# Splitting an expert's 176 hidden units as 128 and 48, and running the down matmuls of tiles in pairs

## The chip, the cores and the metric

The kernel runs on one NeuronCore of one Trainium2 chip. The metric is the device time of one execution in microseconds. Three runs of the kernel before gave 1685.27, 1688.10 and 1691.52 us; the median is 1688.1. A profile is of one further execution.

## The reference, cut to what matters

The model is a two-layer decoder on an input of 16 sequences of 128 tokens, width 256, all in float32. Layer 0 is self-attention with 16 heads, a recurrent mixing over time, and a mixture of experts; layer 1 is self-attention, cross-attention and a quantised feed-forward. The change touches the mixture of experts of layer 0 alone. For each token `h` it computes

```
top4   = the 4 best of 16 experts by router weight
out    = sum over e in top4 of  wt[e] * ( silu(h @ w_gate[e]) * (h @ w_up[e]) ) @ w_down[e]
         + sigmoid(h . sh_gate_w) * ( silu(h @ sh_gate) * (h @ sh_up) ) @ sh_down
w_gate[e], w_up[e]: 256 x 176      w_down[e]: 176 x 256
sh_gate, sh_up:     256 x 704      sh_down:   704 x 256
```

The second line is a "shared expert" that every token goes through. The 176 hidden units of an expert are what the change splits in another way: they are the contracted dimension of the last product, and TensorE contracts over partitions[...].

## The kernel before

The kernel walks through the layers in stages. In the expert stage the tokens have been scattered to a DRAM buffer `hs`, sorted by expert and padded, and a map `tmapT` holds for each of 79 tiles of 128 rows the expert (row 0 of the map) and the first row in `hs` (row 1). 79 is 16 * 4 + 16 - 1 (`NTILES`), the most that the padding can need. Each tile takes five functions:

- `fetch(j)` (L741 to L750) reads the tile's row number from the map into a register of SyncE and lets SyncE's queue load 128 rows from `hs` into `hx`, which has four buffers.
- `turn_in(j)` (L936) transposes `hx` on TensorE into PSUM (`pht`, L940), and ScalarE copies it to `hxT` (L942).
- `inner(j)` (L946) multiplies `hxT` by the expert's gate and up weights, which lie together in `wbig` and are addressed with the expert number in a register of TensorE (`pgu`, L956). ScalarE takes the silu of one half (L961), VectorE multiplies by the other (`eact`, 128 x 176, L963).
- `turn_act(j)` (L966) transposes `eact` in two halves of 88 columns (`pat`, L970), and VectorE copies both with one instruction to `eactT` (L972).
- `outer(j)` (L975) multiplies `eactT` by the expert's down weights (`pey`, L979), two matmuls with 88 rows each that add up in PSUM. ScalarE or VectorE copies the result to `ey` (L985), and SyncE's queue stores it to `hs` in place of the input rows (L987).

All weights of all experts are loaded once, ahead of the stage: gate and up to `wbig` (L689), down to `wd` (L695) as 88 partitions x 16 experts x 2 halves x 256.

The order on TensorE is written out by hand (`manual_schedule`): the loop over steps `s` calls, in this order, `fetch(s)`, `turn_in(s-2)`, `inner(s-3)`, `turn_act(s-5)`, `outer(s-6)` and then `beside(s)`.

```python
for s in range(NTILES + LAG):
    for f, lag in ((fetch, 0), (turn_in, 2), (inner, 3), (turn_act, 5), (outer, LAG)):
        if 0 <= s - lag < NTILES and not (f is fetch and s in where):
            f(s - lag)
    beside(s)
```

`beside(s)` puts other work between the tiles: up to three "chores" a step at first (loads and quantising of layer 1's weights, on VectorE, ScalarE, GpSimd and SyncE's queue), from step 27 on the gathers of finished rows by GpSimd (`back_rows`) and their sums (`back_sums`), and from step 36 on, every second step, a piece of layer 1's self-attention. The other engines' orders are a scheduler's.

The four tiles in PSUM that these functions write (`pht`, `pgu`, `pat`, `pey`) share one pool, `tps`, of four buffers of a bank each, given out in turn; whoever takes a buffer waits until its last content has been read.

One other place matters. The shared expert (`sh_hidden`, `sh_down`, L701 to L735) runs just before, and its 704 units are five chunks of 128 and one of 64. For that one the kernel already puts 64-row matmuls on two row groups of TensorE in turn: partitions 0 to 63 and 64 to 127 (the last chunk of `acc_sh`, L728).

Of the kernel before, what the change touches and what calls it, by code (L numbers as in the profile page):

```python
# [9 lines left out]
F32 = mybir.dt.float32  # L10
# [7 lines left out]
P = 128  # L18
B = 16
S = 128  # L20
D = 256
NK = D // P
# [7 lines left out]
E = 16  # L30
TOPK = 4
IMOE = 176
# [4 lines left out]
NTILES = B * TOPK + E - 1  # L37
# [15 lines left out]
def decoder(ctx, tc, a, out):  # L53
    nc = tc.nc
    V, A, PE, GP = nc.vector, nc.scalar, nc.tensor, nc.gpsimd
# [42 lines left out]
    for r in range(H // 4):  # L98
        hs = slice(4 * r, 4 * r + 4)
# [7 lines left out]
    ident = const.tile([P, P], F32, name="ident")  # L107
# [9 lines left out]
    ET, SPE = mybir.EngineType.PE, mybir.EngineType.SP  # L117
# [219 lines left out]
    hs = dram.tile([ROWS, D], F32, name="hs")  # L337
# [202 lines left out]
    with tc.tile_pool(name="l0", bufs=2, reuse_waits="tile") as wk0:  # L540
        hTs, qTs, kTs, live, accs, norms = {}, {}, {}, {}, {}, {}
# [117 lines left out]
    tps = psum1.enter_context(tc.tile_pool(name="tps", bufs=4, space=PSUM, reuse_waits="tile"))  # L659
# [14 lines left out]
    mp = moestack.enter_context(tc.tile_pool(name="moe", bufs=3, reuse_waits="tile"))  # L674
# [12 lines left out]
    for k in range(NK):  # L687
        for j, name in ((0, "L0_ffn_w_gate"), (1, "L0_ffn_w_up")):
            nc.sync.dma_start(  # L689
                wgu[:, k, :, j * IMOE : (j + 1) * IMOE], a[name][:, k * P : (k + 1) * P, :].rearrange("e p i -> p e i"),  # L690
            )
    HM = IMOE // 2
    wd = mp.tile([HM, E, 2, D], F32, name="wd", bufs=1)
    for j in range(2):
        nc.sync.dma_start(wd[:, :, j, :], a["L0_ffn_w_down"][:, j * HM : (j + 1) * HM, :].rearrange("e p d -> p e d"))  # L695

# [37 lines left out]

    why = "the map holds each of its candidates once"
    NB = 8
    held, where, live = {}, {}, {}

    def fetch(j):  # L741
        row = nc.values_load(
            tmapT[0:1, 1, j : j + 1], engines=[SPE], min_val=0, max_val=ROWS - P, skip_runtime_bounds_check_because=why,
        )
        where[j] = row
        hx = mp.tile([P, D], F32, tag="hx", name="hx", bufs=4)
        ins = nc.sync.dma_start(hx, hs[bass.ds(row, P), :]).ins
        tc.declare_no_dep(ins, group="stores", reason="each tile has rows of its own")
        tc.add_to_no_dep_group("fetches", ins)
        live[j] = hx  # L750

    tmapT = rt.tile([1, 2, P], I32, name="tmapT")
# [43 lines left out]
    def map_and_first():  # L796
        yield from tile_map()
        while scatters:
            yield UNIT
        for j in range(2):  # L800
            fetch(j)
# [162 lines left out]
        live[j] = act  # L964

    def turn_act(j):  # L966
        act = live[j]
        pt = tps.tile([P, NK, P], F32, tag="t", name="pat")
        for k in range(2):
            PE.transpose(pt[:HM, k, :], act[:, k * HM : (k + 1) * HM], ident)  # L970
        aT = mp.tile([HM, 2, P], F32, tag="eactT", name="eactT")
        V.tensor_copy(aT, pt[:HM])  # L972
        live[j] = aT

    def outer(j):  # L975
        aT = live.pop(j)
        py = tps.tile([P, D], F32, tag="t", name="pey")
        for k in range(2):
            ins = PE.matmul(  # L979
                py, aT[:, k, :], wd[:, bass.ds(held[j], 1), k, :].rearrange("p e d -> p (e d)"),  # L980
                start=k == 0, stop=k == 1,
            )
        last_pe[:] = [ins.ins]
        y = mp.tile([P, D], F32, tag="ey", name="ey")
        nc.any.tensor_copy(y, py)  # L985

        ins = nc.sync.dma_start(hs[bass.ds(where[j], P), :], y).ins  # L987
        for group in ("stores", "fetches", "gathers"):
            tc.declare_no_dep(ins, group=group, reason="each tile has rows of its own")
        tc.add_to_no_dep_group("stores", ins)  # L990

# [6 lines left out]
    moments, rows = {}, {}  # L1000
# [54 lines left out]
    for tag in ("hT3", "hg"):  # L1055
        r = rt.tile([P, 2 * H, 32], F32, tag=tag, name="spread")
# [3 lines left out]
    for i in range(2):  # L1060
        r = xa.tile([P, H, 32], F32, tag=f"vaug{i}", name=f"vaug{i}")
# [232 lines left out]
    with tc.issue_after(sh_down.last):  # L1294
        with tc.manual_schedule(engines={ET}):
# [5 lines that stand above are left out]
            load_last_weights()  # L1301
# [12 lines left out]
    kraw, kTs, vs, qTs, sqs, sums, rqs, live, accs = ({} for _ in range(9))  # L1314
# [314 lines left out]
```

## Time and profile before

| what | value |
|---|---|
| median of three runs | 1688.1 us |
| time of the profiled execution | 1678.52 us |
| its span, first to last instruction | 1676.8 us |
| mean granted TensorE clock | 0.987 |
| TensorE matmuls, busy share of the span | 97% |
| VectorE / ScalarE / GpSimd, busy share | 57% / 49% / 34% |
| expert stage, first to last down matmul | 773.4 to 1028.4 us |
| down matmuls `pey` (L979) | 316 records, 82.6 us busy |
| transposes `pat` (L970) | 158 records, 273 ns median |
| copies `eactT` (L972) | 79, 420 ns median |
| copies `ey` (L985) | 75 on ScalarE, 372 ns median; 4 on VectorE, 425 ns |

How to read the lines of a profile. "PE" is TensorE's matmuls and "PEld" its weight loads, which overlap with them; DVE is VectorE, ACT ScalarE, POOL GpSimd, SP SyncE; an engine's name with a q is its queue of issues. A line of the timeline has the start in us from the beginning of the span, the length in us, the engine, the line of the kernel, the operation, output<-inputs, the shape, and how many instructions are merged in it; in brackets stands how long the engine was idle before, and what it waited for. Matmuls are pipelined and the ends of their records are modelled, so a row's own duration is longer than the place that it takes in the stream; the distance from start to start is what counts. A float32 matmul leaves two weight loads and two matmul records (two passes), a transpose one of each. In a shape such as 88*128 the first number is the rows (contracted), the second the columns of the array that are in use.

### The profile page before, as it was taken

Reading aid. Unit: us, or ns where it says so; the run is one execution under the profiler, and the core shown is the slowest. Engines: PE = TensorE matmul, PEld = TensorE weight load, DVE = VectorE, ACT = ScalarE, POOL = GpSimd, SP = SyncE. Lnnn points to the kernel's source line nnn. Section 1 sums busy time; section 2 is a strip of 40 time slices with the busy share of each in tenths; the row PEclk is TensorE's granted clock in tenths of the full one; section 3 lists DMA queues with packets and bytes.
Section 4 is the critical chain, followed back from the end, with each engine's and each line's share of the span. In section 5 each row is a group of like instructions: output and inputs, shape, how many; then the busy total and the mean of one; then the engine's idle time right before and its main releaser. Section 6 shows DMA issues by size and latency. Waiting matters only on the chain.

```text
span 1676.8 us, 27285 instructions
## 1 busy us (share of the span) xinstructions
PE 1620.3 (97%) x9808; PEld 1149.9 (69%) x9808; DVE 950.3 (57%) x2492; ACT 814.3 (49%) x2208; POOL 569.1 (34%) x586
## 2 busy tenths in 40 slices
PE   8999999999999999989999999999999999999996
PEld 4666666666666675546776667777777777777774
DVE  2333476457547665633355546467666666666756
ACT  3444454444444533403444445656666666665553
POOL 2010132135124233131265345654444444432420
PEclk9999999999999999999999999999999999999998
DMA  9990000000000019132543225000000000000000
GB/s 299 403 358 1 0 7 7 14 25 26 0 20 32 13 46 268 23 96 87 154 149 111 88 89 177 17 14 11 8 8 8 7 8 8 8 8 10 4 4 13
DMA packets 91660, 110.22 MB, mean 66 GB/s; under 512 B 8646, under 2 KB 66950, under 8 KB 91526
## 3 DMA queue, kind: packets, MB, share of 16 engines
q1 hardware_dynamic: 83094, 89.55, 16.5%
q0 software_dynamic: 6144, 16.79, 3.2%
q10 hardware_dynamic: 2288, 2.14, 0.4%
q8 instruction: 78, 1.28, 0.3%
q14 instruction: 56, 0.46, 0.1%
HBM read 54.06 MB, written 54.39 MB: 65 GB/s over the span
## 4 chain that ended last, share of the span: by engine, by line
PE 90%; DVE 3%; issue 3%; ACT 2%; POOL 1%; DMA 0%; POOLq 0%; DVEq 0%; ACTq 0%; SPq 0%
PE proj L571 13%; PE acc_x L1419 6%; PE proj L1353 6%; PE projv L590 6%; PE acc_l L169 6%; PE pgu L956 5%; PE pey L979 4%; PE sc L581 3%; PE sc L1384 3%; PE z L619 3%; PE z L1404 3%; PE acc_sh L728 2%; PE pg L709 2%; PE pu L709 2%; PE pk L1319 2%
## 5 line engine op out<-in xcount | busy, mean ns | idle before, releaser
L184 ACT ACTIVATE sc<-sc,nmax 128x128 f32<-128x128 f32 x512 | 199.0, 390 | 160.3 <-DVE nmax L181 130.3
L181 DVE TENSOR_REDUCE nmax<-sc 128x4 f32<-128x512 f32 x128 | 87.4, 683 | 184.9 <-POOL sc L584 183.3
L584 POOL TENSOR_SCALAR_AFFINE_SELECT sc<-sc 128x512 f32<-128x512 f32 x64 | 40.9, 639 | 330.9 <-ACT sc L583 313.7
L1353 PEld LDWEIGHTS proj<-hc,wbig 128*128 128x128 f32 x1024 | 124.0, 192 | 29.2 <-issue 23.4
L125 POOL TENSOR_TENSOR rq<-rq,mhalf 128x4 f32<-128x4 f32 x64 | 67.8, 1059 | 209.3 <-DVE rq L1376 193.2
L1419 PE MATMUL acc_x<-wbig,zT 128*128 128x256 f32 x512 | 124.8, 386 | 0.7 <-ACT zT L1410 0.7
L1353 PE MATMUL proj<-hc,wbig 128*128 128x128 f32 x1024 | 124.6, 275 | 0.1
L571 PE MATMUL proj<-hT,wq 128*128 128x512 f32 x256 | 122.2, 600 | 0.5 <-ACT hT L156 0.5
L590 PE MATMUL projv<-wv,hT 128*128 128x512 f32 x256 | 122.3, 601 | 0.0
L169 PEld LDWEIGHTS acc_l<-wo,zT 128*128 128x128 f32 x512 | 96.7, 190 | 36.8 <-issue 26.8
L169 PE MATMUL acc_l<-wo,zT 128*128 128x256 f32 x512 | 120.9, 379 | 0.0
L571 PE MATMUL proj<-hT,wk 128*128 128x512 f32 x256 | 120.3, 592 | 0.0
L956 PE MATMUL pgu<-wbig,hxT 128*128 x316 | 108.8, 467 | 2.7 <-DVE eactT L972 1.3
L1419 PEld LDWEIGHTS acc_x<-wbig,zT 128*128 128x128 f32 x512 | 93.3, 190 | 23.6 <-issue 11.3
L125 POOL TENSOR_TENSOR ss<-ss,mhalf 128x32 f32<-128x32 f32 x16 | 87.5, 5471 | 45.3 <-DVE ss L1102 45.2
L1213 POOL DMA_INDIRECT back<-hs,idx x64 | 64.1, 1002 | 93.4 <-DMA hs<-ey 46.2
L184 ACT ACTIVATION_READ_ACCUMULATOR sc<-sc,nmax 128x1 f32 x512 | 95.6, 187 | 0.0
L1387 DVE SCALAR_TENSOR_TENSOR sc<-sc,rq,mask 128x128 f32<-128x128 f32 x256 | 77.4, 343 | 28.6 <-PE sc L1384 24.1
L571 PEld LDWEIGHTS proj<-hT,wk 128*128 128x128 f32 x256 | 48.8, 191 | 61.7 <-issue 53.3
L972 DVE COPY eactT<-pat 88x256 f32<-88x256 f32 x79 | 33.0, 418 | 99.4 <-PE pat L970 79.5
L619 PEld LDWEIGHTS z<-probT,v 128*128 128x128 f32 x512 | 67.1, 192 | 29.5 <-issue 28.7
L979 PE MATMUL pey<-wd,eactT 88*128 x316 | 82.6, 384 | 1.6 <-ACT hxT L942 0.9
(342 smaller groups left out, 3508.8 us busy)
## 6 DMA issues: line engine op xcount, KB each, us to landing
hs<-zero SPq DMA_DIRECT2D x16, 2048.0 KB
hx<-hs SPq DMA_DIRECT2D x79, 128.0 KB
hs<-ey SPq DMA_DIRECT2D x79, 128.0 KB
wbig<-in_L_ffn_w_gate_dram SPq DMA_DIRECT2D x2, 1408.0 KB
wbig<-in_L_ffn_w_up_dram SPq DMA_DIRECT2D x2, 1408.0 KB
wd<-in_L_ffn_w_down_dram SPq DMA_DIRECT2D x2, 1408.0 KB
wq<-in_L_attn_W_Q_dram SPq DMA_DIRECT2D x8, 256.0 KB
vT<-in_ctxT_dram ACTq DMA_DIRECT2D x8, 256.0 KB
```

Of the source, the lines that this page charges most:

```text
L125: power.last = GP.tensor_tensor(v, v, mhalf[:, :n], ALU.pow).ins
L169: ins = PE.matmul(acc[:, t, :], zT[:, i, :], w[:, h0 + i, :], start=h0 == 0 and i == 0 and t % 2 == 0, stop=last and i == 3, skip_group_ch ...
L181: softmax.last = V.tensor_reduce(nmax, sc, AX.X, ALU.max, negate=True).ins
L184: A.activation(p[:, i, :], sc[:, i, :], AF.Exp, bias=nmax[:, i : i + 1], accum_out=rs[:, i : i + 1])
L571: PE.matmul(pj, w[:, k, h, :], hTs[g][:, k, :], start=k == 0, stop=k == NK - 1)
L590: PE.matmul(pv, hTs[g][:, k, at], wv[:, k, 4 * hq : 4 * hq + 4, :].rearrange("p h e -> p (h e)"), start=k == 0, stop=k == NK - 1,)
L619: PE.matmul(pz[:, i, :], v[:, i, :], pT[:, i, :], start=True, stop=True)
L956: PE.matmul(pg, hT[:, k, :], wgu[:, k, bass.ds(held[j], 1), :].rearrange("p e i -> p (e i)"), start=k == 0, stop=k == NK - 1,)
L979: ins = PE.matmul(py, aT[:, k, :], wd[:, bass.ds(held[j], 1), k, :].rearrange("p e d -> p (e d)"), start=k == 0, stop=k == 1,)
L1353: PE.matmul(pj[:, i, :], wqx[:, n, k, i * DH : (i + 1) * DH], hTs[b][:, k, :], start=k == 0, stop=k == NK - 1,)
L1387: V.scalar_tensor_tensor(sc[:, i, :], psc[:, i, :], rq[:, i : i + 1], mask, ALU.mult, ALU.add)
L1419: PE.matmul(accs[b][:, :D], zT[:, i, :], wox[:, 4 * n + i, :], start=n == 0 and i == 0, stop=n == NKV - 1 and i == 3,)
```

## The change

The 176 units of an expert are split as 128 and 48 in place of 88 and 88.

- `wd` now holds only the first 128 units' weights of all experts (128 partitions x 16 x 256), loaded with one DMA.
- The weights of the last 48 units are loaded for each tile by `fetch(j)`: it reads the expert number from the map into a second register and issues one more DMA of 48 rows of 1 KB, ahead of the load of `hx`, into `wd2` with eight buffers. For even tiles they go to partitions 0 to 47, for odd tiles to partitions 64 to 111.
- `turn_act` transposes the first 128 columns of `eact`, and then, for an even tile, the last 48 (which land on partitions 0 to 47), and for an odd tile the last 112, so that the last 48 units land on partitions 64 to 111. VectorE copies in two instructions; `eactT` has four buffers in place of three.
- `outer(j)` does nothing for an even tile, except for the last tile (78). For an odd tile it does the pair: the two 128-row matmuls, then the two 48-row matmuls, which lie on different row groups of TensorE; then two copies and two stores. In the loop the pair's matmuls come in the steps with odd `s`, in which `turn_act` treats an even tile; the steps with even `s` have no down matmuls.

```diff
-    HM = IMOE // 2
-    wd = mp.tile([HM, E, 2, D], F32, name="wd", bufs=1)
-    for j in range(2):
-        nc.sync.dma_start(wd[:, :, j, :], a["L0_ffn_w_down"][:, j * HM : (j + 1) * HM, :].rearrange("e p d -> p e d"))
+
+    HR, HO = IMOE - P, P // 2
+    wd = mp.tile([P, E, D], F32, name="wd", bufs=1)
+    nc.sync.dma_start(wd, a["L0_ffn_w_down"][:, :P].rearrange("e p d -> p e d"))
...
     def fetch(j):
...
         where[j] = row
+        e = nc.values_load(
+            tmapT[0:1, 0, j : j + 1], engines=[SPE], min_val=0, max_val=E - 1, skip_runtime_bounds_check_because=why,
+        )
+        r = j % 2 * HO
+        wds[j] = mp.tile([P, D], F32, tag="wd2", name="wd2", bufs=8)
+        nc.sync.dma_start(wds[j][r : r + HR], a["L0_ffn_w_down"][bass.ds(e, 1), P:].rearrange("e p d -> (e p) d"))
         hx = mp.tile([P, D], F32, tag="hx", name="hx", bufs=4)
...
     def turn_act(j):
-        act = live[j]
-        pt = tps.tile([P, NK, P], F32, tag="t", name="pat")
-        for k in range(2):
-            PE.transpose(pt[:HM, k, :], act[:, k * HM : (k + 1) * HM], ident)
-        aT = mp.tile([HM, 2, P], F32, tag="eactT", name="eactT")
-        V.tensor_copy(aT, pt[:HM])
+        act, r = live[j], j % 2 * HO
+        pt = tps.tile([P, 2, P], F32, tag="t", name="pat")
+        PE.transpose(pt[:, 0, :], act[:, :P], ident)
+
+        PE.transpose(pt[: r + HR, 1, :], act[:, P - r :], ident)
+        aT = mp.tile([P, 2, P], F32, tag="eactT", name="eactT", bufs=4)
+        V.tensor_copy(aT[:, 0, :], pt[:, 0, :])
+        V.tensor_copy(aT[r : r + HR, 1, :], pt[r : r + HR, 1, :])
         live[j] = aT
 
     def outer(j):
-        aT = live.pop(j)
-        py = tps.tile([P, D], F32, tag="t", name="pey")
-        for k in range(2):
-            ins = PE.matmul(
-                py, aT[:, k, :], wd[:, bass.ds(held[j], 1), k, :].rearrange("p e d -> p (e d)"),
-                start=k == 0, stop=k == 1,
-            )
+
+        if j % 2 == 0 and j < NTILES - 1:
+            return
+        js = range(j - j % 2, j + 1)
+        pys = [tps.tile([P, D], F32, tag="t", name="pey") for _ in js]
+        for k, n in ((0, P), (1, HR)):
+            for py, j in zip(pys, js):
+                r = j % 2 * HO if k else 0
+                ins = PE.matmul(
+                    py, live[j][r : r + n, k, :],
+                    wds.pop(j)[r : r + n] if k else wd[:, bass.ds(held[j], 1), :].rearrange("p e d -> p (e d)"),
+                    start=k == 0, stop=k == 1,
+                )
         last_pe[:] = [ins.ins]
...
+        for py, j in zip(pys, js):
+            live.pop(j)
+            y = mp.tile([P, D], F32, tag="ey", name="ey")
+            nc.any.tensor_copy(y, py)
+
+            ins = nc.sync.dma_start(hs[bass.ds(where[j], P), :], y).ins
```

More of the change, by code (lines that the diff above doesn't have):

```diff
@@ L738, in decoder @@
     NB = 8
-    held, where, live = {}, {}, {}
+    held, where, live, wds = {}, {}, {}, {}
     def fetch(j):
@@ L983, in outer @@
-        last_pe[:] = [ins.ins]
[L984 to L990, printed above, removed]
+        if j % 2 == 0 and j < NTILES - 1:
+            return
+        js = range(j - j % 2, j + 1)
+        pys = [tps.tile([P, D], F32, tag="t", name="pey") for _ in js]
@@ new lines, in outer @@
+        for k, n in ((0, P), (1, HR)):
[6 more added lines that the diff above has]
+                )
+        last_pe[:] = [ins.ins]
+        for py, j in zip(pys, js):
[3 more added lines that the diff above has]
+            ins = nc.sync.dma_start(hs[bass.ds(where[j], P), :], y).ins
+            for group in ("stores", "fetches", "gathers"):
+                tc.declare_no_dep(ins, group=group, reason="each tile has rows of its own")
+            tc.add_to_no_dep_group("stores", ins)
```

## The prediction

> **What bounds the kernel now.** I read the share of the engines first, then the stretch of the run in which the changed functions work, then one step of that stretch, and last the places where TensorE already works on row groups.
>
> ```profile
> span 1676.8 us, 27285 instructions
> PE 1620.3 (97%) x9808; PEld 1149.9 (69%) x9808; DVE 950.3 (57%) x2492; ACT 814.3 (49%) x2208; POOL 569.1 (34%) x586
> PE 90%; DVE 3%; issue 3%; ACT 2%; POOL 1%; DMA 0%; POOLq 0%; DVEq 0%; ACTq 0%; SPq 0%
> ```
>
> TensorE is busy for 97% of the span and makes up 90% of the chain that ended last. The expert stage runs from 773 to 1029 us. Its three thirds by engine (sum, instruction count, PE first):
>
> ```profile
> 773.50:860.00 86.50, 85.13 (x411) 62.48 (x410) 37.57 (x115) 37.54 (x113) 26.20 (x38) 1.00 0.45 137
> 860.00:944.00 84.00, 80.83 (x510) 57.98 (x509) 45.49 (x130) 36.81 (x93) 47.74 (x40) 1.00 0.38 117
> 944.00:1028.60 84.60, 79.16 (x573) 56.41 (x573) 43.41 (x122) 38.22 (x89) 37.34 (x33) 0.98 0.35 109
> ```
>
> TensorE is idle for 10 of 255 us; VectorE and ScalarE are busy for half or less. So a microsecond of TensorE saved or lost here is a microsecond of the time. One step, with nothing beside it:
>
> ```profile
> 805.91 0.38 PE L940 MATMUL pht<-ident,hx 128*128 128x128 f32 x2
> 806.13 1.35 PE L956 MATMUL pgu<-wbig,hxT 128*128 x4
> 807.32 0.38 PE L970 MATMUL pat<-ident,eact 128*88 128x128 f32 x2
> 807.54 1.03 PE L979 MATMUL pey<-wd,eactT 88*128 x4
> 808.40 0.38 PE L940 MATMUL pht<-ident,hx 128*128 128x128 f32 x2
> ```
>
> The widths overlap, so I take start to start: 0.22 + 1.19 + 0.22 + 0.86 = 2.49 us a tile. A f32 matmul leaves two records (two passes), a transpose one; a pass of 256 columns takes 0.86 / 4 = 0.215 us, and it takes that with 88 rows in use as with 128.
>
> **The down matmuls.** For two tiles the kernel now streams 8 passes, 1.72 us. After the change the two 128-row chunks stream 4 passes (0.86) and the two 48-row chunks stream 4 passes on different row groups. If those overlap, they take the room of two, 0.43. Against that stands what it costs to enter and leave row groups. The shared expert's tail does just this with 64 rows (matmuls, then weight loads with their idle time):
>
> ```profile
> 666.96 0.59 PE L709 MATMUL pu<-hT,wsh 128*128 128x512 f32 x1
> 667.48 1.14 PE L728 MATMUL acc_sh<-wsh,act 64*128 64x256 f32 x8
> 668.55 0.70 PE L709 MATMUL pg<-hT,wsh 128*128 128x512 f32 x1
> ...
> 667.48 0.73 PEld L728 LDWEIGHTS acc_sh<-wsh,act 64*128 64x128 f32 x8 [0.76 <-issue]
> 668.55 0.30 PEld L709 LDWEIGHTS pg<-hT,wsh 128*128 128x128 f32 x2 [0.33 <-issue]
> ```
>
> Eight passes start in four pairs, 7 ns apart within a pair (667.48, 667.80, 668.02, 668.24), so the overlap is real. But the load ahead of them doesn't slip under the matmul before, as others do: it starts at 667.48, and the 512-column pass begun at 666.96 (0.43 long) was through at 667.39. That is 0.09 of waiting, and the first pass streams 0.11 after its load begins: **0.20 to enter**. To leave: 0.09 again, and 0.11 for a load of plain weights, or 0.06 where a transpose follows, as it will here (in this stage the last 32-row pass starts at 908.34, the transpose's load at 908.53, its second pass at 908.70). **0.15 to 0.20 to leave**. The 48-row section then takes 0.20 + 0.43 + 0.15 = 0.78, where the plain form had 0.86: -0.08 a pair (-0.02 with the dearer exit). Over 39 pairs -3.1. The last of 79 tiles has no partner: 0.43 + 0.20 + 0.43 + 0.15 = 1.21 for 0.86, +0.35. Together **-2.8 us**.
>
> Here a rule of the Trainium skill would say more. "TensorE: Matmul & The Clock Gate", section "Measured speedup vs the span model", puts a pack at the duration of one matmul plus 4 ns for each further tile, with no charge for entering. By it the pair would take 0.43, the saving be 39 x 0.43 = 16.8 less 0 for the last, and the time 1671 before any wait. The trace has the 7 ns, but also the 0.35 to 0.41 around the pack, and a pack of two short passes is mostly that. I go by the row.
>
> **The transposes.** Their count stays at two a tile. The second is 48 columns wide for an even tile and 112 for an odd one, against 88; each still streams 128 columns, 0.11. For an even tile one thing is open: does a width under 64 put the array into column groups? The bf16 transpose of 64 columns at L1452 waits like that: its load starts at 1202.28, where the pass begun at 1202.13 was through at 1202.18, and the next full load at 1202.45. Counted as above that is 0.31 for entering and leaving, x40 = +12.4. But "TensorEngine Tiling (Array Packing)", section "Restrictions", says that column tiling disables the transpose mode for FP32 input, and these are FP32 transposes with the one record each of that mode. By the rule 0, by the row +12.4. The row is bf16, no f32 transpose under 88 wide is in this trace: I take 0 and keep 12.4.
>
> **VectorE.** One eactT copy (0.42 mean, 88x256) becomes two. The nearest half-width row that reads PSUM is 128x128 at L1387, 0.34: two are at most 0.68, +0.26 x 79 = 20 us on an engine idle for 128 of these 255 us. What matters is the odd tile's copy, which is used one step later. A step without down matmuls is now only 0.22 + 1.19 + 0.22 = 1.63 long; 0.68 plus 0.2 of latency fits. At 0 on the path; with VectorE late by over 0.7 it would show.
>
> **ScalarE and PSUM.** Two ey copies (0.37) come together after the pair, and the next transposed input (hxT) queues behind both. Before, hxT ended 0.85 after its transpose began (806.76), while its matmul came at 2.71; now 0.85 + 0.37 = 1.22, while the matmul comes 1.85 after. The margin falls from 1.86 to 0.63. Of the four PSUM buffers two go to a pair at once, so the second must wait for hxT of the same step: 1.22 against 0.22 + 1.19 + 0.22 + 0.43 = 2.06. No wait, with 0.8 to spare. The chores on ScalarE (0.54 quantised weights, table loads 1.28) are about as long as these margins: between 0 and +6 us; I take **+2**, 20 late steps by 0.1.
>
> **SP's queue.** Per tile it now issues one more register load and one more DMA, ahead of the hx load, in order with the stores:
>
> ```profile
> 806.33 0.33 SPq L747 DMA_DIRECT2D hx<-hs  x1
> 806.90 0.35 SPq L987 DMA_DIRECT2D hs<-ey  x1
> 808.82 0.33 SPq L747 DMA_DIRECT2D hx<-hs  x1
> ```
>
> After the first of these the queue stores (0.35), reads the row number (TENSOR_LOAD, 0.27), does its address registers, and stands ready at 807.81: 1.48 of 2.49 used, the rest waiting for an hx buffer. The change adds 0.27 + 0.05, some 0.2 of registers and 0.36: 0.88, so 2.36 of 2.45. It fits, barely, and hx has four buffers, so a load may come several steps late before TensorE waits. The 48 KB themselves have six steps. Cost 0; bounds 0 and +9 (2.7 a tile over the first 36 steps, where nothing else lengthens a step). The gathers on POOL wait for stores (46.2 us of "hs<-ey"), and a pair's second store leaves some 0.7 later; POOL is busy for 111 of 255. Nothing.
>
> **Memory.** wd falls from 32 to 16 KB a partition, the per-tile weights add 8, the fourth eactT 1, so the shared expert's weights lie 7 KB lower, and their load may wait for other tiles than `SPq L680 <- PE z L619`. That load is not what the first shared matmul waits for (631.66): its semaphore was up at 628.69, and the residual sum at L634, over at 631.60, came last. 0, between -4 and +3.
>
> **The sum.** -2.8 + 2 = -0.8. The profiled execution took 1678.52 (span 1676.8 and 1.7 around it), 9.6 below the median of the runs; I lay the difference on the median: 1688.1 - 0.8 = **1687.3**. Faster or slower by 0.5%, 8.4 us, is about what a measurement of this kernel can tell from no change.
>
> **Rivals.** (1) *The short step.* hxT is ready only 0.63 before its matmul. If ScalarE or SP runs later than that, TensorE stands at L956 in every second step. Each 0.1 us costs 3.9 over 39 pairs; from a mean wait of 0.29 a pair (11.2 over 39: the 8.4 and the 2.8 saved) it is slower by more than 8.4. At 0.4 it ends at 1688.1 - 2.8 + 15.6 = 1700.9. For it: the bare margin and SP at 96%. Against: TensorE's waits for other engines sum to some 9 us in 255 now. (2) *Column groups for 48-wide transposes*: 1699.7. (3) *The pack doesn't overlap* (the change doesn't do what it says): two more passes, 39 x 0.43 = +16.8, 1704; the 7 ns of L728 speak against it. (4) *Entering and leaving hides* behind waits TensorE has anyway: up to 39 x 0.35 less, 1673.6. Against: 4% idle.
>
> **Chances.** About even 0.47, with a range of its own of 1681 to 1696; (1) 0.20, (2) 0.08, (3) 0.07; (4) and an earlier start of the shared expert together 0.18. So faster 0.18, same 0.47, slower 0.35. The range must leave out 0.2: 1676 cuts half of (4), 1702 the top of (1) and most of (3).
>
> **What would show it.** Right: pey in two shapes, 128 rows and 48 rows, the latter's records in pairs a few ns apart; the loads ahead of them and the pht loads behind idle 0.3; two steps in 4.9 us around 800. Rival 1: idle time before pgu at L956 or pht at L940 put down to ACT hxT or to the hx DMA. Rival 2: the load of a 48-wide pat starting 0.09 after the array is through. Rival 3: four 48-row passes 0.215 apart. What makes me wrong first is the margin of the short step, then the price of entering a row group right after matmuls whose address comes from a register, which no row here shows.

## The result and the profile after

The changed kernel takes **1698.35 us** (median of five runs, 1696.11 to 1702.08), the kernel before 1688.1 (five runs, 1680.47 to 1691.52): a ratio of 1.0064, 95% interval 1.0045 to 1.0084, so 10 us slower. The forecast was 0.8 us faster; the range given with it (1676 to 1702) holds the time, but the interval leaves out both the forecast and no change. The experiments ran in five sets, and the kernel before differs by up to 29 us between them (1686.9, 1657.6, 1658.3, 1686.4 and 1658.4 us), so every run below is set against the kernel before of its own set.

The page of the changed kernel: span, busy time of the engines, and the engines' shares of the chain that ended last.

```profile
span 1694.4 us, 27623 instructions
PE 1620.6 (96%) x9808; PEld 1134.9 (67%) x9808; DVE 965.5 (57%) x2575; ACT 811.2 (48%) x2204; POOL 567.6 (33%) x586
PE 86%; DVE 5%; issue 3%; POOL 1%; ACT 1%; DMA 1%; another core or an unknown queue 1%; SPq 1%; POOLq 0%; DVEq 0%; ACTq 0%
```

TensorE's busy time is what it was (1620.3 before), and the span is longer: the loss is waiting. Of the 17.6 us between the two spans 6.9 lie ahead of the expert stage, whose first `pht` starts at 773.57 after 766.66; the change is not needed to explain them, for in a later trace of the kernel before the stage starts as late (z0, below). The stage itself takes 272.4 us, 262.1 before. Here it is in three stretches that hold the same tiles in every kernel, tiles 0 to 47, 48 to 77 and the last one (length, busy time and count of TensorE, weight loads, VectorE, ScalarE, GpSimd, then granted clock, DMA share, GB/s). The changed kernel:

```profile
773.57:909.42 135.85, 121.19 (x577) 78.40 (x575) 62.63 (x217) 51.22 (x153) 47.48 (x58) 0.99 0.47 142
909.42:1026.56 117.14, 112.69 (x827) 75.88 (x825) 71.14 (x214) 56.51 (x132) 57.48 (x45) 1.00 0.37 113
1026.56:1046.00 19.44, 17.15 (x121) 11.11 (x119) 10.66 (x28) 5.05 (x13) 6.51 (x9) 0.82 0.67 229
```

and the kernel before in a later run (w0, below), in which the granted clock is 1.00 in the first two stretches:

```profile
751.99:874.34 122.35, 119.96 (x576) 87.62 (x575) 55.64 (x171) 51.93 (x154) 47.33 (x58) 1.00 0.46 142
874.34:989.54 115.20, 113.74 (x825) 82.48 (x824) 65.91 (x183) 56.68 (x133) 56.85 (x46) 1.00 0.34 102
989.54:1007.03 17.49, 16.76 (x123) 11.90 (x122) 9.04 (x22) 6.46 (x15) 8.57 (x9) 0.90 0.64 223
```

Tiles 0 to 47 went from 122.35 to 135.85 us. TensorE was idle for 2.4 of these 122 and is idle for 14.7 of the 136. These are the steps in which TensorE has the least work beside the tiles. The rest of the stage adds 1.9 and 2.0. Against the trace that the forecast was read from, tiles 0 to 47 add nearly as much (122.9 there), but that trace has 123.4 in the second stretch, with 4.3 us of waits for ScalarE's hxT and 3.4 us at half clock; so its stage as a whole is only 10.3 us shorter.

The longest of TensorE's waits in the stage of the changed kernel (sum in us, times, longest). `raw`, `wdq` and `wsum` belong to the quantising of layer 1's weights, `spread` and `pqT` to layer 1's attention:

```profile
PE pht L946 <- DMA hx<-hs: 6.5, 5, 1.9
PE pqT L1125 <- DVE spread L1130: 4.8, 5, 1.9
PE pey L992 <- ACT hxT L948: 3.1, 3, 1.6
PE wsum L896 <- DVE wgqs L889: 1.6, 1, 1.6
```

and of the kernel before (w0):

```profile
PE pey L979 <- ACT hxT L942: 0.9, 4, 0.2
PE pqT L1109 <- DVE spread L1114: 0.7, 1, 0.7
```

The first line of the changed kernel has no counterpart before. TensorE's own step is as forecast. One undisturbed pair in the timeline (start, length), with the down matmuls of the pair ahead of it:

```profile
794.35 1.66 PE L992 MATMUL pey<-wd,eactT 128*128 x8
795.95 0.44 PE L946 MATMUL pht<-ident,hx 128*128 128x128 f32 x2
796.22 1.35 PE L962 MATMUL pgu<-wbig,hxT 128*128 x4
797.40 0.27 PE L975 MATMUL pat<-ident,eact 128*128 128x128 f32 x1
797.51 0.27 PE L977 MATMUL pat<-ident,eact 128*112 128x128 f32 x1
797.62 0.38 PE L946 MATMUL pht<-ident,hx 128*128 128x128 f32 x2
...
799.13 0.27 PE L977 MATMUL pat<-ident,eact 128*48 128x128 f32 x1
799.25 1.66 PE L992 MATMUL pey<-wd,eactT 128*128 x8
```

From 795.95 to 799.25 it is 3.30, and a section of eight passes takes 1.60 (794.35 to 795.95): 4.90 us for two tiles, against 4.98. A transpose of 48 columns starts 0.12 ahead of the next instruction, one of 112 0.11. A few steps later the DMA queue of SyncE (SPq) and TensorE:

```profile
805.66 0.36 SPq L753 DMA_DIRECT2D hx<-hs  x1
806.59 0.35 SPq L751 DMA_DIRECT2D wd<-in_L_ffn_w_down_dram  x1
807.43 0.33 SPq L753 DMA_DIRECT2D hx<-hs  x1
807.86 0.39 SPq L936 DMA_DIRECT2D raw<-in_L_ffn_w_upT_dram  x1
808.50 0.95 SPq L1003 DMA_DIRECT2D hs<-ey  x2
810.30 0.35 SPq L751 DMA_DIRECT2D wd<-in_L_ffn_w_down_dram  x1
811.17 0.35 SPq L753 DMA_DIRECT2D hx<-hs  x1
812.10 0.33 SPq L751 DMA_DIRECT2D wd<-in_L_ffn_w_down_dram  x1
812.92 0.33 SPq L753 DMA_DIRECT2D hx<-hs  x1
813.50 0.96 SPq L1003 DMA_DIRECT2D hs<-ey  x2
814.58 0.41 PE L946 MATMUL pht<-ident,hx 128*128 128x128 f32 x2 [1.73 <-DMA hx<-hs]
815.08 0.35 SPq L751 DMA_DIRECT2D wd<-in_L_ffn_w_down_dram  x1
815.93 0.35 SPq L753 DMA_DIRECT2D hx<-hs  x1
```

From the hx load at 805.66 to the second next at 811.17 the queue takes 5.51 us for two tiles and one chore (raw); without a chore, from 811.17 to 815.93, it takes 4.76. TensorE needs 4.90. The matmuls at 814.58 belong to tile 16, whose load was issued at 811.17, 3.4 us ahead; by its semaphore it had landed at 814.44. In the kernel before the same tile's load was issued 9.55 us ahead. In tiles 12 to 27 this lead is 8.4 to 9.8 us before and 2.1 to 5.2 in the changed kernel, in which most of these loads took 2.0 us to land and this one 3.3. A stop of the queue is enough to use the lead up: at 793.8 it came to the stores of a pair whose copies were not done, stood still for 2.9 us and then for 0.9, and the lead fell from 4.8 us (tile 11) to 2.1 (tile 12). With 4.76 of 4.90 us in use the queue wins it back only where TensorE itself is late.

### The profile page after: what moved, and what is told of

Read it like the earlier page. It is cut to its first block, busy times and chain, and to the rows that moved or that the text cites. A ratio compares the mean times of both kernels' runs of the same rounds, so it can differ in the third digit from the quotient of the medians.

```text
span 1694.4 us, 27623 instructions
## 1 busy us (share of the span) xinstructions
PE 1620.6 (96%) x9808; PEld 1134.9 (67%) x9808; DVE 965.5 (57%) x2575; ACT 811.2 (48%) x2204; POOL 567.6 (33%) x586
## 4 chain that ended last, share of the span: by engine, by line
PE 86%; DVE 5%; issue 3%; POOL 1%; ACT 1%; DMA 1%; another core or an unknown queue 1%; SPq 1%; POOLq 0%; DVEq 0%; ACTq 0%
PE proj L571 13%; PE acc_x L1435 6%; PE projv L590 6%; PE proj L1369 6%; PE acc_l L169 6%; PE pgu L962 4%; PE sc L581 3%; PE sc L1400 3%; PE z L619 3%; PE z L1420 3%; PE pey L992 3%; PE acc_sh L728 2%; PE pg L709 2%; PE pu L709 2%; PE pk L1335 2%
## 5 line engine op out<-in xcount | busy, mean ns | idle before, releaser
L1406 POOL TENSOR_TENSOR sc<-sc,rsum 128x512 f32<-128x512 f32 x64 | 66.8, 1044 | 38.3 <-DVE rsum L1405 19.1
L521 POOL DMA_INDIRECT hs<-hg,idx x64 | 63.9, 998 | 44.9 <-DVE idx L514 27.9
```

## The experiments

Two causes were to be told apart at first: the work on SyncE's queue (register load and tail load for each tile), and the pairing itself. Differences are of medians within the set; the ratio and its interval follow. Each run has a name of two characters, x1 to w1.

**The change without the loads, and the loads without the change.**

```diff
-        wds[j] = mp.tile([P, D], F32, tag="wd2", name="wd2", bufs=8)
-        nc.sync.dma_start(wds[j][r : r + HR], a["L0_ffn_w_down"][bass.ds(e, 1), P:]...)
+        wds[j] = wd8[:, 0, :]   # loaded once, expert 0, rows 0-47 and 64-111; no register load
```

> The changed kernel without the per-tile loads: one expert's 48 tail rows are loaded once, at both partition offsets, and every tile's second product reads those (so the down projection of 15 of the 16 experts is computed with another expert's tail). TensorE's instructions, their order and the memory layout stay those of the changed kernel. Theory A (SyncE's queue: the register load and the load of the tail ahead of each hx make hx late): the expert stage falls from 272.4 us by 11 to 13 us, to 259-262, the hx waits of TensorE vanish, and the time is 1684-1688. Theory B (the pairing itself, with both pey of a pair and their two copies at once, makes the stage long): the stage stays at 270-273 and the time at 1697-1700. The 4 us later start of the shared expert's first matmul stays under both if it is a matter of where tensors lie.

Measured (x1): 1690.12 against 1686.93, +3.2 us (1.0016, 1.0006 to 1.0027). The hx waits are gone. Two variants of the changed kernel in the same set, x2 and x3 below, stand at +11.4 and +11.5: taking the loads away gives back 8 of 11 us.

```diff
+        e = nc.values_load(tmapT[0:1, 0, j : j + 1], engines=[SPE], ...)
+        wd2 = mp.tile([P, D], F32, tag="wd2", name="wd2", bufs=1)
+        nc.sync.dma_start(wd2[:48], a["L0_ffn_w_down"][bass.ds(e, 1), 128:]...)
         hx = mp.tile([P, D], F32, tag="hx", name="hx", bufs=4)
```

> The kernel before, with 88 and 88 rows as it was, and only the SyncE part of the change added: for each tile the expert's number is read into a register and the 48 rows are loaded into a buffer that nothing reads, ahead of hx. No wait for a free buffer comes with it. Theory A2 (a full queue): the stage grows by 8 to 11 us, 1696-1700. Theory A1 (only the buffer wait hurts): within 2 us of before, 1687-1690. Theory B (pairing): no change, 1687-1689.

Measured (x4): 1700.1, +13.2 (1.0080, 1.0064 to 1.0097), as much as the whole change. So the loads alone make the kernel slower. With one buffer for all of them a load has to wait until the one ahead has landed: 3.0 us of such waits in four places, which the expectation had left out, so a little of the 13.2 may be this run's own. Both were run once more, in another set:

> Again the changed kernel without per-tile loads (one expert's tail rows for every tile). Without the loads there remain: pairs in two buffers +4.9, shorter products 39 x -0.09 = -3.5, the lone last tile +0.35, and, if VectorE's second copy is on the path, +2 to +3. Sum: +2 without that copy, +4 to +5 with it (1.001 to 1.003 of before). If the loads were not what costs, it stays at 1.008 to 1.010.

> Again the kernel before with the per-tile register load and tail load added on SyncE ahead of hx, into a buffer that nothing reads. If the loads cost what is missing (14.8 measured, less 4.9 for the pairs, plus 3.5 for the shorter products, less 2.5 for the copies): +10 to +13. If they only cost where the clock drops anyway: +0 to +5.

Measured (z1, z3): +3.0 (1.0023, 1.0008 to 1.0038) and +13.2 (1.0089, 1.0070 to 1.0107). Where do 13 us come from when TensorE's list has no wait for hx? In the trace of z3 two pairs of tiles of the first 48 take 12.6 and 13.5 us, where before they take 5.1 and 6.7, and nearly all others what they took before. The first one (SPq, VectorE, TensorE):

```profile
815.91 0.88 SPq L834 DMA_DIRECT2D gh<-in_L_attn_g_head_dram  x2
818.05 0.16 DVE L1054 TENSOR_TENSOR gh<-gh 128x1 f32<-128x1 f32 x1 [6.83 <-DMA gh<-in_L_attn_g_head_dram]
819.09 0.41 DVE L977 COPY eactT<-pat 88x256 f32<-88x256 f32 x1
819.56 2.71 PE L961 MATMUL pgu<-wbig,hxT 128*128 x4 [5.43 <-DVE eactT L977]
```

gh is four small loads of 16 numbers for the next layer. VectorE's instruction for it stands ahead of an eactT copy in VectorE's order, and waits 6.83 us for the last of the four; the copy waits with it, then TensorE for 5.43. In the kernel before (the first trace), these loads stand behind the 6th to 8th hx load in SyncE's instruction order (issued from 769.1 to 772.3, waited for 1.3); with the fuller queue the order written out by the scheduler has them behind the 17th to 21st (804.2 to 816.4), among steps that leave SyncE no time. In the changed kernel they stand behind the 12th to 14th, and VectorE waits 4.0. The clock drops with it (windows of z3; the granted clock is the third number from the right):

```profile
803.00:816.00 13.00, 11.13 (x55) 8.12 (x53) 2.66 (x8) 5.02 (x16) 0.00 (x0) 1.00 0.56 169
816.00:823.00 7.00, 3.44 (x8) 2.20 (x9) 2.78 (x11) 0.32 (x1) 0.00 (x0) 0.53 0.35 109
```

In the second pair TensorE waits 4.5 us for spread, which needs a 5.47 us instruction of GpSimd; in GpSimd's order this stands behind four gathers, the first of which waits for a store of SyncE's queue:

```profile
891.74 1.18 POOL L1218 DMA_INDIRECT back<-hs,idx  x1 [4.61 <-DMA hs<-ey]
896.70 5.47 POOL L125 TENSOR_TENSOR ss<-ss,mhalf 128x32 f32<-128x32 f32 x1
```

So the loads can cost in two ways that these runs do not separate: SyncE's queue is fuller when it runs, and the scheduler writes the chores into it in another order. A kernel with the loads and with gh kept where it was has not been run.

**Is it the tail buffers, or where tensors lie?**

```diff
-        wds[j] = mp.tile([P, D], F32, tag="wd2", name="wd2", bufs=8)
+        wds[j] = mp.tile([P, D], F32, tag="wd2", name="wd2", bufs=16)
```

> The changed kernel with 16 buffers for the tail rows instead of 8. Theory A1 (it is the wait for a free buffer, with hx queued behind it: 39 us of such waits stand in SyncE's queue): most of the stage's loss goes, 1687-1690. Theory A2 (SyncE is simply full in the dense part, 4.77 us of issuing per pair against TensorE's 4.90, and chores push it over): the buffer waits vanish but hx is as late in the dense part, 1695-1699. Theory B (pairing): 1697-1700. As the 8 KB also move the shared expert's weights back to about where they lay before, its first matmul would start 4 us earlier under the layout theory, in any case.

Measured (x2): 1698.35, +11.4 (1.0071, 1.0053 to 1.0088). The wait for a free tail buffer is gone from the list, the hx waits of TensorE turn into one of 3.4 us behind VectorE (again the gh loads, now issued until 819.6) and one of 7.6 for spread, and the time stays. The buffers are not the cause.

```diff
+    pad = mp.tile([P, 1792], F32, name="pad", bufs=1)
+    V.memset(pad[:, :1], 0.0)
```

> The changed kernel with an unused tile of 7 KB per partition ahead of the others (one column of it is set once), which puts the shared expert's weights back where they lay before. Layout theory (the shared expert's weights came to lie on memory that is freed at another time, so that its first matmul starts at 637.3 instead of 631.7 us): the start returns to 632-633 and the time falls by 4 to 5 us, to 1693.5-1694.5. Rival (the start differs from execution to execution, or by the PE queue's own state): the start stays at 636-638 or the time within 1.5 us of 1698.4.

Measured (x3): 1698.42, +11.5 (1.0068, 1.0050 to 1.0085); the first shared matmul starts at 638.4. So the place of the weights is not the cause. The kernel before, traced again, has the same late start, 8 us between its last acc_l and that matmul:

> The kernel before, unaltered, once more, for its trace beside the others of this call. Where the clock holds in the shared expert's stage, its expert stage should take 253 to 256 us instead of the 262.1 of the trace that was predicted from (two waits of 1.5 and 2.3 us and 3.4 us at half clock stood in that one).

Measured (z0): 1685.9, -0.5 (0.9998, 0.9982 to 1.0014), first shared matmul 8.3 us after the last acc_l, expert stage 265.2. The expectation of 253 to 256 did not apply: the clock did drop ahead of the stage. The stage starts at 773.4 here, as in the changed kernel (773.6), and at 766.7 in the trace that the forecast was read from. That one was a quick execution, and the 6.9 us between the two need no change to explain them.

**Moving the loads instead of removing them.**

```diff
     def fetch(j):
         row = nc.values_load(...)
+        hx load
         e = nc.values_load(...)
         wds[j] load
-        hx load
```

> The changed kernel with one change of order: each tile's hx is loaded ahead of its register load and tail load, not behind them. SyncE's work stays the same, and the wait for a free tail buffer now stands behind hx. Theory A (hx is late because of what is queued ahead of it): each hx leaves 1 us earlier, the hx waits of the dense part shrink to one or two, and the time is 1690-1695. If SyncE is so full that the order doesn't matter, 1697-1699.

Measured (x8): +13.2 (1.0084, 1.0071 to 1.0098). The changed kernel itself in the next set:

> The changed kernel once more, unaltered, to stand on the same chip as the three beside it (chips differ by 30 us in the time of the kernel before). On the first chip it took 1.0064 of before. Expected here: 1.005 to 1.009 of before; the loads taken off SyncE ought to be worth 8 to 11 us of it.

Measured (y0): 1673.08 against 1658.25, +14.8 (1.0089, 1.0074 to 1.0103). So the order is worth little, 1 to 2 us with intervals that overlap: TensorE's hx waits are 1.5 us in sum (3.8 in y0), but the gh loads stand behind the 13th to 17th hx load, VectorE waits 3.7 us for them, and TensorE 5.6 in sum for spread. Here the full queue delayed what now stood last in it.

```diff
-        e = nc.values_load(..., engines=[SPE], ...)
-        nc.sync.dma_start(wds[j][r : r + HR], ...)
+        e = nc.values_load(..., engines=[mybir.EngineType.Pool], ...)
+        nc.gpsimd.dma_start(wds[j][r : r + HR], ...)
```

> The changed kernel with each tile's register load and tail load moved from SyncE's queue to GpSimd's; the rest is unaltered. Theory A (what hurts is the work ahead of hx in SyncE's queue): TensorE's hx waits vanish and the time falls towards that without per-tile loads, +3 to +5 us against before. Rival (GpSimd's own queue, whose gathers and conversions have waiters, takes over the lateness: 79 loads at about 1 us each beside 120 us of work): +10 us or more.

Measured (y3): +16.2 (1.0096, 1.0081 to 1.0111): the rival. TensorE waits for no hx, the gh loads are early again, and instead GpSimd's loads (512 ns each, 53.8 us of waiting for pey to free a tail buffer ahead of them) stand in front of what VectorE and ScalarE need from it: TensorE waits 4.6 us at once for spread and 3.1 for hxT. The same rows are still moved, so it was not their transfer that made hx late but their place in SyncE's queue.

**The pairing alone.**

```diff
-        py = tps.tile([P, D], F32, tag="t", name="pey")
-        for k in range(2):
+        js = range(j - j % 2, j + 1)       # only at odd j
+        pys = [tps.tile([P, D], F32, tag="t", name="pey") for _ in js]
+        for k in range(2):                 # both chunks of 88 rows
+            for py, j in zip(pys, js):
```

> The kernel before with its two 88-row chunks, all weights resident and no added load, and only the pairing added: both tiles' second products are multiplied at the odd tile, the two first chunks ahead of the two second ones, and both copies and stores follow. Theory P (the pairing itself costs: two pey and their copies at once in four PSUM buffers): this is where the 3 us by which the kernel without per-tile loads stood above the one before come from, together with the 3 us that the shorter products ought to have given: 1689-1693. The prediction's own term for it was +2 us (1688-1690). Rival (pairing costs nothing, the 48-row products give back less than counted): 1686-1688.

Measured (x5): 1662.45 against 1657.58, +4.9 (1.0028, 1.0018 to 1.0038). At tiles 28 and 29 (GpSimd, ScalarE, TensorE):

```profile
833.52 0.95 POOL L1220 DMA_INDIRECT back<-hs,idx  x1 [0.30 <-issue]
834.54 1.20 POOL L860 TENSOR_SCALAR raw<-raw 128x448 f32<-128x448 f32 x2
835.13 0.58 ACT L907 ACTIVATE wdq<-raw 128x448 bf16<-128x448 f32 x1 [3.58 <-POOL raw L860]
835.61 0.35 ACT L942 COPY hxT<-pht 128x256 f32<-128x256 f32 x1
836.02 2.37 PE L983 MATMUL pey<-wd,eactT 88*128 x8 [2.98 <-ACT hxT L942]
```

GpSimd does four gathers and only then the next piece of raw; ScalarE's conversion waits for that piece, hxT stands behind it in ScalarE's order, and TensorE's pey waits until hxT has freed a PSUM buffer for the pair. The clock is halved for 3.4 us soon after this wait of 2.98. In the kernel before, one pey at a time needs one buffer and meets the same conversion with a wait of 0.64. The pair in one buffer (the first matmul starts both halves):

```diff
-        pys = [tps.tile([P, D], F32, tag="t", name="pey") for _ in js]
+        both = tps.tile([P, 2, D], F32, tag="t", name="pey")
+        pys = [both[:, i, :] for i in range(len(js))]
-                    start=k == 0, stop=k == 1,
+                    start=k == 0 and j == js[0], stop=k == 1, skip_group_check=True,
-            nc.any.tensor_copy(y, py)
+            A.copy(y, py)
```

> The kernel with the two 88-row chunks in pairs (4.9 us slower than before on its chip), with both products of a pair in the two halves of one PSUM buffer instead of in two of the four buffers, and both copies on ScalarE. Theory P (a pair takes two of the four PSUM buffers, so that a late ScalarE reaches TensorE: the 3.0 us wait of pey for hxT at tile 30 and the 1.3 us at wsum): most of the 4.9 us goes, -1 to +2 us against before. Rival (the pairs cost by the order of the copies and stores, not by buffers): +4 to +6.

Measured (y1): +1.4 (1.0004, 0.9995 to 1.0012). TensorE's pey no longer waits, while the waits for wsum (1.3) and spread (2.0) stand in this trace too. The scheduler's order moved with it, with the pieces of raw now ahead of the gathers, and both copies are on ScalarE, so the run shows buffers and order together. With one copy of 128x512 per pair besides:

```diff
-            y = mp.tile([P, D], F32, tag="ey", name="ey")
-            A.copy(y, py)
+        ys = mp.tile([P, 2, D], F32, tag="ey", name="ey", bufs=2)
+        A.copy(ys[:, : len(js)], both[:, : len(js)])
```

> As the one-buffer pairs, with one copy of 128x512 out of PSUM instead of two of 128x256, by the rows of the trace 0.59 us instead of 2 x 0.37 us (the second copy of a pair so comes earlier and the first later; both stores follow it; two 2 KB ey buffers instead of three of 1 KB, and three eactT buffers). Theory P: as the kernel beside it, or 0 to 2 us less: -2 to +1 us against before. If copies and stores in pairs are what costs: +3 to +6.

Measured (y2): -0.5 (0.9997, 0.9988 to 1.0005), not told from before. No version beat the kernel before.

**The price of the 48-row products.**

```diff
+    wdt = mp.tile([HR, E, D], F32, name="wdt", bufs=1)   # all tails, rows 0-47
-        for k in range(2):
+        for k, n in ((0, P), (1, HR)):                      # no pairs
-                py, aT[:, k, :], wd[:, bass.ds(held[j], 1), k, :]
+                py, aT[:n, k, :], (wdt if k else wd)[:, bass.ds(held[j], 1), :]
```

> 128 and 48 rows, all tails resident on rows 0 to 47 (no added load), and no pairing: each tile's 48-row product runs alone, right after its 128-row one. By the row of the trace that the prediction used (0.20 us to enter and 0.15 us to leave a stretch of fewer rows) each of 79 tiles pays 0.35 us: +27 us, 1712-1716. If entering and leaving cost nothing, 1686-1689; if they hide half the time behind other work, about 1700.

Measured (x6): +21.8 (1.0134, 1.0118 to 1.0149). Two undisturbed tiles take 5.67 us against 4.98: 0.345 a tile, the 0.35 of the row. For 79 tiles that is 27 us. TensorE is idle 2.2 us less in the stage than in w0; where the other 3 us went is not shown.

```diff
-                r = j % 2 * HO if k else 0
+                r = 0                              # pairs, both tails on rows 0-47, resident
```

> As the changed kernel, in pairs, but all tails resident on rows 0 to 47 and both 48-row chunks on the same row group, so that they cannot run side by side, and no added load. Against the kernel without per-tile loads (1690.1) this prices the overlap: by the row, four passes of 0.215 us more for each of 39 pairs, 33 us of passes halved to 16.8: 1705-1708. If the two row groups did not overlap in the first place, within 2 us of 1690.

Measured (x7): +21.9 (1.0145, 1.0124 to 1.0166), 1.2% above the kernel without loads, about 20 us by the two ratios, whose intervals add up to some 5 us either way. An undisturbed pair takes 5.32 against 4.89 with two row groups (z1): 0.43, just two passes, 16.8 us for 39 pairs. First x6 for one tile, then x7 for a pair:

```profile
779.46 0.60 PE L983 MATMUL pey<-wd,eactT 128*128 x2
779.98 0.70 PE L983 MATMUL pey<-wdt,eactT 48*128 x2
780.61 0.44 PE L942 MATMUL pht<-ident,hx 128*128 128x128 f32 x2
```

```profile
783.33 1.03 PE L988 MATMUL pey<-wd,eactT 128*128 x4
784.29 1.13 PE L988 MATMUL pey<-wdt,eactT 48*128 x4
785.35 0.44 PE L942 MATMUL pht<-ident,hx 128*128 128x128 f32 x2
```

The 48-row section is 0.63 for two passes and 1.06 for four.

**VectorE's second copy.**

```diff
-        V.tensor_copy(aT, pt[:HM])
+        for k in range(2):
+            V.tensor_copy(aT[:, k, :], pt[:HM, k, :])
```

> The kernel before with one edit: eactT is copied out of PSUM in two copies of 88x128 (by the rows 0.29 us each) instead of one of 88x256 (0.42 us). The prediction costed it at 0 on the path, at most 0.68 us: +0 to +0.7. Rival (VectorE is on the path in the part with the pieces, where TensorE waits for spread and z): +2 to +3.

Measured (z2) on the kernel before: +5.0 (1.0043, 1.0028 to 1.0059), the rival and more. But in pairs (the one-buffer kernel with the same edit):

> The pairs of 88-row chunks in one PSUM buffer (+0.7 us against before), with eactT copied in two copies of 88x128 instead of one of 88x256. If the copies cost in pairs what they cost without (+5 to +7): +5 to +8 against before. If in pairs only the waits for spread and z show it (0.3 each, some 9 of them): +3 to +4. If pairs hide it: +0 to +1.5.

Measured (w1): -0.7 (0.9996, 0.9986 to 1.0005). In pairs the second copy is hidden; unpaired it is not. Which of the unpaired kernel's waits carries the 5 us was not settled: TensorE's waits for VectorE's eact come 9 times there, but sum to only 1.8 us, and the traced executions of z2 and z0 differ by 0.8 us alone (1689.2 and 1688.4). The kernel before beside w1:

> The kernel before, unaltered, for its trace beside the one of this call. If the clock holds in the shared expert's stage (start within 1.5 us of the last acc_l, stage of 125 us), its expert stage should take 253 to 256 us; else 262 to 265.

Measured (w0): 1656.82 (one run), first shared matmul 1.4 us after the last acc_l, expert stage 255.0. Against the 268.3 of y0 (another set, the clock at 1.00 in the stage ahead as well) the change costs 13.2 us in the stage, 11.2 of them in tiles 0 to 47.

## Why the prediction was wrong

**The step that failed** is "SP's queue": "It fits, barely, and hx has four buffers, so a load may come several steps late before TensorE waits ... Cost 0; bounds 0 and +9". Its rate was right: 2.36 a tile was worked out, 4.76 / 2 = 2.38 measured, of 2.45. The conclusion was not. A queue at 97% has no room for what else passes through it: raw and the gh loads at 0.37 to 0.50 each, and the waits of stores for their copies. The count was of fetches and stores alone. And the four buffers did not cover the lateness: in the kernel before they allowed a lead of 8.4 to 9.8 us, in the changed one it stays at 2.1 to 5.6 in tiles 4 to 47, and a stop of the queue takes it down to the 2.0 that a load needs to land. Besides hx only the tail rows and the gathers were asked after, and both put at nothing. What became late differs from kernel to kernel: hx (the changed one), gh, with VectorE and eactT behind it (x2, z3), stores, with gathers and spread behind them (z3). Measured cost: +13.2 on the kernel before, twice, and 8 taken back from the changed one, so around or above the upper bound. That the loads cost this is shown; how much of it is the full queue and how much the scheduler's new order is not.

Rival 1 came nearest, at a chance of 0.20: it named SP's queue and, as a sign, waits of `pht` put down to the hx DMA, which are there. But it reckoned with a small wait in every second step, and found are five waits of 0.8 to 1.9 us and others behind other engines. That its 1700.9 lies close to 1698.35 is in part luck.

**A term mis-sized**: the pair in PSUM. "No wait, with 0.8 to spare", then +2 as "20 late steps by 0.1". Measured +4.9, with one long wait of 3.0 at tiles 28 and 29 and 3.4 us at half clock after it, which by an estimate from these two figures is 2.3 us more than the 0.64 before and another 1.7, so 4.0 of the 4.9. The waits for wsum and spread are longer too (1.3 and 1.5), but y1, y2 and w1 have such waits as well (1.3 and 2.0) and are not told from before. The margin was worked out against ScalarE's own instructions; ScalarE there waits for GpSimd.

**What was right.** The passes: -0.08 a pair was forecast, 4.98 to 4.90 measured in the changed kernel and 4.89 in z1, so 39 pairs give -3.1 to -3.5 us. The row of the trace against the rule of the pack: x6 pays 0.345 a tile for entering and leaving, and x7 shows that the overlap is full, 0.43 a pair; the rule's 16.8 us are the overlap without that price. The transposes: 0, no sign of column groups. VectorE at 0 on the path: right in pairs (w1), but by luck of the order rather than by the argument, since the same idle engine showed the copy in the unpaired kernel (z2). Memory at 0: right (x3, z0).

**The sum again**, with measured terms: -3.5 for the passes, +0.35 for the lone tile (x6's price of one tile), +4.9 for the pairs, +8 to +13 for the loads: +10 to +15. Measured: +10.3 in the first runs, +14.8 in y0's set. The terms don't add exactly: the changed kernel without loads should stand at +1.8 and stands at +3.0 to +3.2.

One combination was left out: 128 and 48 with every expert's last rows resident at both places, and the pair in one PSUM buffer. From y2 (-0.5), the passes (-3.1) and the lone tile (+0.35) it would be an estimated 3 us faster than before; no run shows it.

## What to carry to other kernels

A queue that is close to full by a steady count should be costed as a cause of delay, not as hidden: list everything else that passes through it, ask how it would win back a lead once lost, then ask of each engine which instruction waits for the last of these and what stands behind that instruction. A change that streams less on the engine that sets the time can still lose, when its price is paid on an in-order queue that feeds this engine. Buffers taken two at a time need a margin against the longest stall of whoever frees them, not against that engine's own durations.

## What the runs showed of the hardware

**Long waits came with a slower clock.** Each of TensorE's ten waits of 2.98 us or more in tiles 0 to 47 overlapped with, or was followed within 2 us by, 3.4 or 6.8 us at half the full clock: 3.06 (x1), 3.39 and 7.57 (x2), 4.48 and 6.24 (x4), 2.98 (x5), 3.11 and 4.62 (y3), 5.43 and 4.50 (z3, the first the row with 0.53 above). Of shorter ones some were (1.73 at 814.58 in the changed kernel, 2.02 in y1, 2.29 in y0), others not (2.94 in z1, 2.72 in x8, 2.00 in w1). So a long wait costs more than its own length: 3.4 us at half clock are an estimated 1.7 us of matmuls lost.

**The shared expert's stage, which nobody changed, has two lengths.** In the same kernel it takes 125 us at a granted clock of 1.00, starting 1.4 us after the last acc_l (w0), or 138.0 at 0.94, starting 8.3 us after (z0):

```profile
627.10:635.40 8.30, 0.41 (x2) 0.01 (x1) 0.69 (x1) 0.00 (x0) 6.17 (x8) 0.72 0.97 340
635.40:773.40 138.00, 128.71 (x470) 74.94 (x470) 67.24 (x156) 35.37 (x48) 31.52 (x34) 0.94 0.37 102
```

All twenty traces have about 125 us, or 135 to 138. This makes up some 20 of the 29 us between the sets. Why the clock drops in one set and not in another, the runs do not say; the number of the chip does not settle it, for x1 to x4 and y0 to y3 carry the same one (5) and show the one and the other. A difference of two traces taken apart can so hold microseconds that no edit made.
